# Layer 0 of a two-layer network on one Trainium2 core: the router's input of six batches turned by VectorE and DMA instead of TensorE

## The chip, the core and the metric

The kernel runs on one core of one Trainium2 chip. The core's engines work side by side, each through its own instructions in order: TensorE (PE in the profile, with its weight loads as PEld), VectorE (DVE), ScalarE (ACT), GpSimd (POOL) and SyncE (SP), which here only issues transfers (DMA). They wait for each other by semaphores. The metric is the device time of one execution in microseconds (us). Before the change it is 2221.11 us, the median of three runs (2220.45 to 2225.37).

## What is computed

Eight sequences (batches) of 512 tokens with 512 features, in f32, pass two layers. In each layer an attention and a feed-forward part follow each other, each with a residual sum and a layer norm behind it. Layer 0 alone matters here:

```python
x = L0_attn_x                                    # (8, 512, 512)
q, k, v = (x @ W.T + b for each of WQ, WK, WV)   # 16 heads of 32
attn = softmax(causal(q @ k.T / sqrt(32))) @ v
x = layernorm(x + attn @ WO.T + bO)
router_logits = x @ gate_weight.T + x @ (2 * gate_lora_B @ gate_lora_A).T   # 8 experts
weights, selected = top_k(softmax(router_logits), 2)
x = layernorm(x + sum of the two selected experts, weighted)
```

The experts' weights each have a low-rank addition (their adapters), which the kernel adds into the weights while the attention runs. Layer 1 is another attention and a quantised feed-forward part; the change does not touch it.

## The kernel before

All of layer 0's attention is in `attention0` (L1214). It walks over the eight batches `b`, in each over four groups `g` of four heads, and in each group over three units `u` of key tiles (`UNITS = ((0,), (1, 3), (2,))`): 12 units a batch, written (g, u) below. A unit is, on TensorE:

- `scores` (L1348): the products of queries and keys into one psum tile `sc` with a single buffer; ScalarE takes the exponential into `p` (L1360), GpSimd sets the masked corner to zero (L1365);
- whatever `plan` (L1410) put into this unit;
- `product` (L1370) of the unit before: `av`, four matmuls side by side for the four heads (L1380); VectorE adds the unit's `p` to the group's total (L1388);
- in a group's second unit, `normalise` (L1391) of the group before: row sums `rs` (L1395), a copy by ScalarE into `r_inv` (L995), VectorE's reciprocal (L1398) and product `aoT` (L1399), and a sum by GpSimd for a guard (L998).

`plan` is an order written by hand: a dictionary from (g, u) to the pieces to be done there. The framework's scheduler settles the order of instructions from it, for the most part as written, and moves small pieces between neighbouring ones. The pieces of batch `b`:

- `value` (L1282), `query` (L1289) and `key` (L1297): four matmuls each of 128x512, four values a batch and a query and key for each group, made a group ahead. VectorE adds the bias to the query (L1294), ScalarE to the key (L1302);
- for the batch before, `pb = b - 1`: four `project` (L1305), which multiply by WO and add to x (L1309); the last one also does the layer norm (`Env.layernorm`, L173: statistics L180 and L181, GpSimd's rstd L182 and L183, the normalising L185) and stores the rows (L188, four transfers);
- then four `turn` (L1315), each with four transposes by TensorE of 128x128 (L1320), which VectorE and ScalarE in turn copy from psum into `x1T` (L194, L192): the router needs x with the features on the partitions;
- `score` (L1326): the logits from `x1T` (L491), copied by ScalarE (L1330); `choose` (L1332): the best two experts of each token, one product (L503) and a long row of small instructions on VectorE;
- for the batch before that, `dispatch`, `one_hot` and `enter`: a table of which token goes where (L547 to L590); its one-hot rows use the same room as `x1T`, which has one buffer;
- two `merge` (L1404): two adapter products each (L781), scaled by ScalarE into buffers with the tag `r_inv` (L792), added to the expert weights by GpSimd (L794). The tag `r_inv` has two buffers, shared with the normalisation.

All psum tiles other than `sc` and `av` (v, q, k, projections, turns, logits, adapters, row sums) share the two buffers of the tag `mm`: each allocation waits until the one two before it has been copied out. SyncE loads the next batch's transposed input (L1244) and its rows x (L1248); x has two buffers, so the load for `b + 1` waits for the last reader of batch `b - 1`. GpSimd adds the bias row to x (L1474) once it has landed.

The file has a class `Turn` (L73) that layer 1's attention already uses: VectorE transposes 32x32 blocks (L88), four DMAs write them to DRAM with their blocks in another order (L93), and one DMA brings them back (L96). Its tokens then lie in another order within the batch, which `by_tile` (L98) puts right by an access pattern.

## Time and profile before

| what | value |
|---|---|
| median of the runs, us | 2221.11 |
| profiled execution, us | 2228.55 |
| its span on the core, us | 2226.8 |
| mean granted clock of TensorE | 0.993 |
| TensorE's batches 2 to 7 in the span, us each | 90.8, 93.5, 96.3, 93.5, 92.9, 93.3 |
| transposes by TensorE into `x1T` (L1320) | 128, recorded at 273 ns |
| transfers: x, 1 MB; `turned` in layer 1, 256 KB; the way back, 1 MB | 7.5, 4.1 and 4.8 us from issue to landing |

The profile is one execution taken by the hardware profiler. Its page lists the busy time of each engine; further views list waits (who waited for whom, how often and how long), instructions in order of time (start, length, engine, line, operation, output<-input, number of records) and transfers. A 128x512 matmul in f32 leaves two records. Consecutive matmuls overlap, so the sum of lengths is more than the time from the start of one to the start of the next. A batch is measured here from the first score of its first unit to that of the next batch. Layer 0's attention covers the first 760 us of the span.

### The profile page before, as it was taken

The page shows a single profiled execution, that of the slowest core. Times are in us where ns is not written, and L with a number is a line of the kernel's source. Part 1 is how long each engine was busy: PE and PEld are TensorE (multiplying, and loading weights), DVE is VectorE, ACT ScalarE, POOL GpSimd, SP SyncE. Part 2 cuts the span into 40 slices and gives each one's busy share as a digit, 9 for nine tenths or more (in the row PEclk, how much of TensorE's full clock was granted, in tenths as well). Part 3 has the DMA queues.
Part 4 walks back from the last instruction along what each step waited for, and adds up shares of the span by engine and source line. Part 5 has one row for each costly group of instructions (what it writes and reads, how often), then busy time and mean ns, then how long its engine had stood idle before and what let it go on. Part 6 is the DMA issues. An engine that isn't in the chain of part 4 may idle for free. (4 is left out here: it accounts for less than half of the span.)

```text
span 2226.8 us, 23678 instructions
## 1 busy us (share of the span) xinstructions
PE 2191.9 (98%) x9006; PEld 1116.6 (50%) x9006; DVE 1273.7 (57%) x2032; ACT 632.0 (28%) x917; POOL 487.6 (22%) x489
## 2 busy tenths in 40 slices
PE   9999999999999999999999999999999999999997
PEld 3344444444444444444443333333343778888876
DVE  3556666666666633323316887798757655555443
ACT  2332323323233232122124333223332222222222
POOL 2322423234132333122105222222211000000000
PEclk9999999999999899999999999999999999999999
DMA  8010101101022216888735212312110321111000
GB/s 297 20 57 1 57 10 48 58 1 58 5 71 94 85 57 181 227 218 214 191 114 193 80 57 86 95 55 77 45 32 13 109 78 57 57 57 57 20 20 21
DMA packets 146428, 182.20 MB, mean 82 GB/s; under 512 B 60530, under 2 KB 89202, under 8 KB 144514
## 3 DMA queue, kind: packets, MB, share of 16 engines
q1 hardware_dynamic: 135024, 144.91, 21.0%
q0 software_dynamic: 10560, 34.61, 5.5%
q8 instruction: 74, 1.21, 0.2%
q10 hardware_dynamic: 722, 1.07, 0.1%
q14 instruction: 48, 0.39, 0.1%
HBM read 117.38 MB, written 63.18 MB: 81 GB/s over the span
## 5 line engine op out<-in xcount | busy, mean ns | idle before, releaser
L903 PE MATMUL ps_gu<-experts,xrT 128*128 128x512 f32 (+1 forms) x520 | 248.8, 601 | 0.0
L1360 ACT ACTIVATE p<-sc 128x2048 f32<-128x2048 f32 (+1 forms) x96 | 152.8, 1592 | 190.0 <-PE sc L1356 183.1
L1148 DVE SCALAR_TENSOR_TENSOR hT<-ps_u,vec,sg 128x512 f32<-128x512 f32 x88 | 65.6, 745 | 195.2 <-PE ps_u L1143 195.2
L1365 POOL TENSOR_SCALAR_AFFINE_SELECT p<-p 128x512 f32<-128x512 f32 x128 | 91.6, 729 | 385.2 <-ACT p L1360 378.5
L1159 PE MATMUL ps_f<-ffn_w,h_half 128*128 128x512 f32 x672 | 170.2, 394 | 0.6 <-issue 0.4
L998 POOL TENSOR_TENSOR g_total<-g_total,r_inv 128x512 f32<-128x512 f32 x64 | 89.7, 1401 | 358.3 <-DVE r_inv L1735 283.0
L1705 ACT ACTIVATE p<-sc 128x1024 f32<-128x1024 f32 x128 | 124.0, 1021 | 105.9 <-PE sc L1702 100.8
L1735 DVE RECIPROCAL r_inv<-r_inv 128x512 f32<-128x512 f32 x32 | 107.1, 3346 | 78.8 <-ACT r_inv L995 78.8
L1388 DVE TENSOR_TENSOR p<-p 128x1536 f32<-128x1536 f32 (+2 forms) x96 | 129.4, 1348 | 39.2 <-POOL p L1365 22.2
L905 DVE TENSOR_TENSOR h<-ps_gu,h 128x256 f32<-128x256 f32 x67 | 28.4, 424 | 212.8 <-ACT h L904 212.8
L903 PEld LDWEIGHTS ps_gu<-experts,xrT 128*128 128x128 f32 x520 | 96.2, 197 | 89.7 <-issue 89.5
L1159 PEld LDWEIGHTS ps_f<-ffn_w,h_half 128*128 128x128 f32 x672 | 124.4, 188 | 33.0 <-DVE h_half L1154 5.6
L1143 PE MATMUL ps_g<-x_high,ffn_w 128*128 128x512 f32 x352 | 138.9, 395 | 0.8 <-DVE x L1676 0.8
L1143 PE MATMUL ps_g<-x_low,ffn_w 128*128 128x512 f32 x352 | 139.1, 395 | 0.0
L1143 PE MATMUL ps_u<-x_low,ffn_w 128*128 128x512 f32 x352 | 138.8, 394 | 0.0
L1143 PE MATMUL ps_u<-x_high,ffn_w 128*128 128x512 f32 x352 | 138.7, 394 | 0.0
L919 PE MATMUL ps_y<-experts,hT 128*128 128x512 f32 (+1 forms) x272 | 127.9, 593 | 0.5 <-ACT hT L913 0.5
L1702 PE MATMUL sc<-qT,kT 64*128 64x512 f32 x512 | 127.3, 615 | 1.0 <-ACT qT L1609 0.7
L1292 PE MATMUL ps_q<-experts 128*128 128x512 f32 x256 | 121.1, 615 | 4.4 <-DMA experts<-in_xT 4.4
L1724 PE MATMUL av<-p,v 128*64 128x512 f32 x512 | 123.8, 605 | 0.0
L1285 PE MATMUL ps_v<-experts 128*128 128x512 f32 x256 | 118.0, 609 | 3.3 <-DVE v L1287 3.3
L1670 PE MATMUL ps_o<-attn_out,aoT 128*128 128x512 f32 x256 | 117.9, 605 | 0.8 <-ACT r_inv L995 0.8
(262 smaller groups left out, 3438.5 us busy)
## 6 DMA issues: line engine op xcount, KB each, us to landing
results<-y SPq DMA_DIRECT2D x68, 256.0 KB, 2.3
turned<-turned SPq DMA_DIRECT2D x56, 256.0 KB, 4.1
pair<-xrT SPq DMA_DIRECT2D x25, 512.0 KB, 3.4
xrT<-pair SPq DMA_DIRECT2D x100, 128.0 KB, 4.5
x<-in_x SPq DMA_DIRECT2D x8, 1024.0 KB, 7.5
experts<-in_gate_up SPq DMA_DIRECT2D x8, 1024.0 KB, 10.8
rows<-x SPq DMA_DIRECT2D x32, 256.0 KB, 2.0
x<-rows SPq DMA_DIRECT2D x8, 1024.0 KB, 15.5
```

Source lines behind the costliest of these rows:

```text
L903: nc.tensor.matmul(ps, lhsT=xT[:, c, :], rhs=self.weights(i, c), start=c == 0, stop=c == ND - 1)
L919: self.nc.tensor.matmul(ps, lhsT=hT[:, c, :], rhs=self.weights(i, ND + c), start=c == 0, stop=c == self.NI - 1)
L1143: nc.tensor.matmul(ps, lhsT=w[:, ts(dc, P)], rhs=x[:, dc, :], start=(dc, i) == (0, 0), stop=(dc, i) == (ND - 1, 1))
L1159: self.nc.tensor.matmul(os[t], lhsT=h[:, ts(t, P)], rhs=self.weights(2 * NHID + c), start=(c, i) == (0, 0), stop=(c, i) == (NHID - 1, 1))
L1285: nc.tensor.matmul(ps, lhsT=xts[b][:, c, ts(t, P)], rhs=wv[:, c, :], start=c == 0, stop=c == ND - 1)
L1292: nc.tensor.matmul(ps, lhsT=wq[:, g, ts(c, P)], rhs=xts[b][:, c, :], start=c == 0, stop=c == ND - 1)
L1360: nc.scalar.activation(p, sc[:, :, :width], AF.Exp, scale=scale)
L1388: nc.vector.tensor_tensor(total[:, :, P * kt :], total[:, :, P * kt :], p[:, :, at : at + w], ALU.add)
L1670: nc.tensor.matmul(ps, lhsT=state[b]["aoT"][:, c, ts(t, P)], rhs=w_out[:, c, :], start=c == 0, stop=c == ND - 1)
L1702: nc.tensor.matmul(sc[:, j, :], lhsT=st["kT"][hs, ts(kt, P)], rhs=st["qT"][g][hs, :], start=True, stop=True)
L1705: nc.scalar.activation(p, sc, AF.Exp, scale=scale)
L1724: nc.tensor.matmul(st["av"][HD * j : HD * (j + 1), :], lhsT=st["v"][:, kt, HD * j : HD * (j + 1)], rhs=p[:, j, :], start=kt == 0, stop=kt ...
```

## The change

Batches 0 to 5 (`by_blocks = NB - 2`) no longer use `turn`. A new `blocks(b)` does what layer 1 does: four block transposes by VectorE into `x1T`, four DMAs to DRAM and one back into the same tile. The logits of these batches are put in the old order of tokens by the access patterns of ScalarE's copy. Batches 6 and 7 are turned by TensorE as before.

The pieces are laid out anew in the plans of batches 1 to 6 (`by_dma`), each of which treats the batch before it:

- projections: from (1,0), (1,0), (1,1), (1,2) to (1,0), (1,1), (1,2), (2,0);
- turning: from two pieces in (2,1) and two in (2,2) to `blocks` in (2,1);
- logits from (3,0) to (3,1), choice from (3,1) to (3,2);
- adapters ("merge"): from ahead of the other pieces in (2,0) and (3,0) to behind the key in (2,2) and behind the logits in (3,1);
- the next batch's first query: from (3,1) to (3,0).

The query of the fourth group in batches 1 to 6 gets its bias from ScalarE instead of VectorE. On SyncE's queue the five new transfers follow the stores of the rows; the load of the next batch's x stands between the four writes and the way back.

```diff
@@ query
-            nc.vector.tensor_scalar(q, ps, vec[:, V_BQ + g : V_BQ + g + 1], None, ALU.add)
+            if g == ND - 1 and 0 < b <= by_blocks:
+
+                nc.scalar.activation(q, ps, AF.Identity, bias=vec[:, V_BQ + g : V_BQ + g + 1])
+            else:
+                nc.vector.tensor_scalar(q, ps, vec[:, V_BQ + g : V_BQ + g + 1], None, ALU.add)
...
+        by_blocks = NB - 2
+        turns = Turn(env, dram, NT, "turned0")
+
+        def room(b):
+            x1Ts[b] = work.tile([P, ND, S], F32, tag="x1T", name="x1T")
+
+        def blocks(b):
+            room(b)
+            flat = x1Ts[b].rearrange("p k s -> p (k s)")
+            for t in range(NT):
+                turns.blocks(flat, t, xs[b][:, t, :])
+            turns.out(flat)
+            turns.back(flat)
...
@@ score
-            nc.scalar.copy(logits[b], ps)
+            if b < by_blocks:
+                nc.scalar.copy(turns.by_tile(logits[b], False), turns.by_tile(ps, True))
+            else:
+                nc.scalar.copy(logits[b], ps)
...
@@ plan
+            pb, last = b - 1, b == NB - 1
+            by_dma = 0 <= pb < by_blocks
...
-                    todo[g, 1].append(lambda nb=nb, ng=ng: query(nb, ng))
+                    todo[g, 0 if by_dma and ng == 0 else 1].append(lambda nb=nb, ng=ng: query(nb, ng))
...
-                places = ((1, 0), (1, 0), (1, 1), (1, 1) if last else (1, 2))
+                places = ((1, 0), (1, 1), (1, 2), (2, 0)) if by_dma else ((1, 0), (1, 0), (1, 1), (1, 1) if last else (1, 2))
...
-                places = ((2, 0),) * 4 if last else ((2, 1), (2, 1), (2, 2), (2, 2))
-                for c, slot in enumerate(places):
-                    todo[slot].append(lambda c=c: turn(pb, c))
-                todo[(2, 1) if last else (3, 0)].append(lambda: score(pb))
-                todo[(2, 2) if last else (3, 1)].append(lambda: choose(pb))
+                if by_dma:
+                    todo[2, 1].append(lambda: blocks(pb))
+                else:
+                    for c in range(ND):
+                        todo[2, 0].append(lambda c=c: turn(pb, c))
+                todo[(3, 1) if by_dma else (2, 1)].append(lambda: score(pb))
+                todo[(3, 2) if by_dma else (2, 2)].append(lambda: choose(pb))
                 if not last:
-                    todo[2, 0].append(merge)
-                    todo[3, 0].append(merge)
+                    todo[2, 2 if by_dma else 1].append(merge)
+                    todo[3, 1].append(merge)
```

The transfers it calls:

```python
    def out(self, room):
        for i in range(self.N):
            src = room[32 * i : 32 * (i + 1), :].rearrange("r (k j f) -> r k j f", j=self.N, f=self.n * 32)
            self.nc.sync.dma_start(out=self.dram.rearrange("(j r) k i f -> r k j i f", j=self.N)[:, :, :, i, :], in_=src)

    def back(self, room):
        self.nc.sync.dma_start(out=room, in_=self.dram.rearrange("p k i f -> p (k i f)"))
```

More of the change, by code (lines that the diff above doesn't have):

```diff
@@ L1313, in attention0 @@
         x1Ts, logits = {}, {}
+        by_blocks = NB - 2
[9 more added lines that the diff above has]
+            turns.back(flat)
         def turn(b, c):
             if c == 0:
-                x1Ts[b] = work.tile([P, ND, S], F32, tag="x1T", name="x1T")
+                room(b)
             ps = mm([P, S], "ps_x1T")
@@ L1417, in plan @@
                 if nb < NB:
-                    todo[g, 1].append(lambda nb=nb, ng=ng: query(nb, ng))
+                    todo[g, 0 if by_dma and ng == 0 else 1].append(lambda nb=nb, ng=ng: query(nb, ng))
                     todo[g, 2].append(lambda nb=nb, ng=ng: key(nb, ng))
-            pb, last = b - 1, b == NB - 1
             if b:
-                places = ((1, 0), (1, 0), (1, 1), (1, 1) if last else (1, 2))
+                places = ((1, 0), (1, 1), (1, 2), (2, 0)) if by_dma else ((1, 0), (1, 0), (1, 1), (1, 1) if last else (1, 2))
                 for t, slot in enumerate(places):
                     todo[slot].append(lambda t=t: project(pb, t))
-                places = ((2, 0),) * 4 if last else ((2, 1), (2, 1), (2, 2), (2, 2))
-                for c, slot in enumerate(places):
-                    todo[slot].append(lambda c=c: turn(pb, c))
-                todo[(2, 1) if last else (3, 0)].append(lambda: score(pb))
-                todo[(2, 2) if last else (3, 1)].append(lambda: choose(pb))
+                if by_dma:
[5 more added lines that the diff above has]
+                todo[(3, 2) if by_dma else (2, 2)].append(lambda: choose(pb))
                 if not last:
-                    todo[2, 0].append(merge)
-                    todo[3, 0].append(merge)
+                    todo[2, 2 if by_dma else 1].append(merge)
+                    todo[3, 1].append(merge)
             if b == 0:
```

## The prediction

> **What bounds the kernel now.** I read the page first, for the share of each engine; then TensorE's waits in the first 760 us, which hold layer 0's attention; then the timelines of one batch, engine by engine. The page:

> ```profile
> PE 2191.9 (98%) x9006; PEld 1116.6 (50%) x9006; DVE 1273.7 (57%) x2032; ACT 632.0 (28%) x917; POOL 487.6 (22%) x489
> ```

> TensorE's waits in 0 to 760 us (total, times, longest):

> ```profile
> PE sc L1356 <- ACT p L1360: 5.2, 7, 1.8
> PE ps_q L1292 <- DMA experts<-in_xT: 4.4, 1, 4.4
> PE ps_v L1285 <- DVE v L1287: 3.3, 4, 1.7
> ```

> The reader sees 98% and, in 760 us, waits of a few us: here the end moves with what TensorE is given, plus the waits a change makes. The fourth batch (267 to 364 us), where the third one's rows are turned; columns are start, length, engine, line, operation and records:

> ```profile
> 327.82 1.14 PE L1356 MATMUL sc<-q,k 32*128 32x512 f32 x8
> 328.78 1.02 PE L781 MATMUL ps_lora<-lora 16*128 16x512 f32 x4
> 329.74 0.64 PE L1380 MATMUL av<-p,v 128*32 128x256 f32 x8
> 330.96 1.15 PE L1356 MATMUL sc<-q,k 32*128 32x384 f32 x16 [0.58 <-ACT p L1360]
> 332.04 3.70 PE L1292 MATMUL ps_q<-experts 128*128 128x512 f32 x8
> 335.57 0.60 PE L1320 MATMUL ps_x1T<-ident,x 128*128 128x128 f32 x4
> 336.10 1.04 PE L1380 MATMUL av<-p,v 128*32 128x512 f32 x2
> 337.08 0.66 PE L1320 MATMUL ps_x1T<-ident,x 128*128 128x128 f32 x4
> ...
> 343.70 0.60 PE L1320 MATMUL ps_x1T<-ident,x 128*128 128x128 f32 x4
> 344.23 0.83 PE L1380 MATMUL av<-p,v 128*32 128x384 f32 x2
> 344.99 0.66 PE L1320 MATMUL ps_x1T<-ident,x 128*128 128x128 f32 x4
> 345.58 1.06 PE L1380 MATMUL av<-p,v 128*32 128x384 f32 x14
> ```

> Tails overlap, so I take costs from start to start. The turns also split the products (av): two records alone take 0.98 us (336.10 to 337.08), while all eight of an unbroken set, at 317.26, take 0.88.

> **What goes.** In unit (2,1) (second of the three units of the third head group) turns, products and sums run from 335.57 to 339.51, 3.94 us; the same products and sums unbroken, in unit (1,1), 317.26 to 319.11, 1.85. The turns cost 2.09. In (2,2) it is 343.70 to 346.57, 2.87, against 326.82 to 327.82, 1.00: 1.87. Together 3.96 us a batch, of which only 2.24 are the turns themselves (0.53 + 0.59, twice). In the built order a projection of 3.53 us stands in (2,0) between that unit's scores and the next, so the wait of 0.58 at 330.96 goes too.

> [...]

> **What moves on TensorE.** Projections, the next batch's query, logits and the choice's product (0.89) keep their lengths. The second adapter pair breaks the scores of (3,1) now (1.92 us instead of 1.08) and breaks that unit's products afterwards. I take the same 0.84; from nothing to 1.1, the larger break in (2,1), is possible, so the ends are +0.8 and -0.3 us. The first pair goes behind the key in (2,2): its second product needs the psum buffer of that key, two allocations back, and ScalarE frees it 0.69 us (k rows) after the key ends, while the first adapter takes 0.48 and the copy starts some 0.2 late: a new wait of about 0.45. So 3.96 + 0.58 - 0.45 = 4.1; adding whole units the same way gives 3.95. I use **4.0 us a batch, 24 in six**.

> **What must hide.** I set the batch's clock to 0 at the start of unit (1,0), 298.66 in the trace. Units afterwards: (1,0) 5.2, (1,1) 11.7, (1,2) 8.7, (2,0) 5.2, (2,1) 6.5, (2,2) 6.7, (3,0) 5.2. So the last projection ends at 30.2, (3,1) begins at 49.2, and its logits want the turned rows at **50.2**.

> The way to them: add, statistics, mean 1.63 us (327.53 to 329.16 before), 1.47 until rstd is there; normalising starts at 33.4. Next, the rows from VectorE's timeline, the first of this batch, the others in layer 1:

> ```profile
> 330.63 4.14 DVE L185 TENSOR_SCALAR x<-x,mv,rstd 128x512 f32<-128x512 f32 x4 [1.48 <-POOL rstd L183]
> ...
> 1258.20 1.92 DVE L746 TENSOR_SCALAR xn<-x,mv,dev 128x512 f32<-128x512 f32 x4
> 1260.03 2.48 DVE L88 STREAM_TRANSPOSE turned<-xn 128x512 f32<-128x512 f32 x4
> ```

> The 4.14 lie beside GpSimd's two adapter sums (2.84 us from 331.65), which move away; two masks (1.22) stay. So 1.9 to 4.1, likely 2.9; blocks 2.5 to 2.7. They end at 37.8 to 40.2, likely 38.9. Then SyncE's queue, as layer 1 does the same transfers:

> ```profile
> 1262.54 3.26 SPq L93 DMA_DIRECT2D turned<-turned  x4
> 1269.11 0.35 SPq L96 DMA_DIRECT2D hT<-turned  x1
> ```

> Four writes, then the way back 6.6 us after the first; it lands 4.8 later (median of its issues), so 11.4 after the blocks. Here the next batch's 1 MB load of x is issued between the two. It lands 5.2 to 7.5 us after issue elsewhere, moving its bytes in about 3. At 343.89 and 345.68 two such loads ran one after the other, so I let x follow the writes: it is done some 9.3 after the blocks and pushes the return by 0.4. Landing is 11.8 after the blocks: 49.6 to 52.0, likely 50.7. The logits wait 0 to 1.8, likely 0.3 to 0.5 (I take 0.3, the nearer to the rows without GpSimd). Behind that wait on TensorE stand the adapters, products and sums of (3,1) and the whole next batch.

> **Other queues.** VectorE loses a query copy (0.75) and two copies of turned rows (1.36) and gains the blocks: +0.4 to 0.6 us a batch in 93, idle for a third of it. What lies behind the blocks is the add (1.7 to 2.1), the reciprocal (3.34) and GpSimd's sum (1.5) that frees r_inv for the second scaled adapter. That ends at about 45.5, ScalarE copies until 46.2, then the exponential of (3,0) takes 1.88: 48.1, and the scores of (3,1) want it at 49.2. One us of cover; if it is gone, a late normalising costs the scores what it would cost the logits, not both. ScalarE loses two copies (0.59 each) and gains the query (0.69); the reordering logits copy has no row: between the plain 0.58 and twice that, with a quarter product in front of the waiting adapter; 0 to 0.6 a batch, I take 0 as the plain copy is the same size. On GpSimd the addition to x (4.53) begins when x has landed, 48.7 instead of 54.7 on this clock; masks and adapter sums follow until 55.9, and the sums' copy, wanted at 55.1, is a us late as it was before (1.79 <-POOL experts at 359.18), with a key of 3.5 behind it as cover. The choice comes one unit later and ends VectorE's chain at about 68.2 on the clock; the values that want its copy come at 70.9. Before, the copy was late by 0.55 behind this batch and by 1.7 ahead of it; I count neither back. SyncE's other issues are behind the return: the load of xT, at 45.2 before and 46 now, needed a batch later.

> **Sum.** 6 x (4.0 - 0.3) = 22.2 us. The profiled execution took 2228.55 us around a span of 2226.8: 2204.6 for the span, 2206.4 for the run. It lies 7.4 above the median of the runs, 2221.11, which I move by the same amount: **2199 us**.

> **Rivals.** (A) The forecast, 2193 to 2205: waits of 0 to 1.3 a batch give 16 to 24 us back, and 3 to 4 more if the value waits shrink. For it: a TensorE that hardly waits loses work. Chance 0.60. (B) The turned rows land late by 1.5 to 3 us: normalising takes its 4.14, or x and the writes share. Of 4.0 a batch 1 to 2.5 stay, 6 to 15 us: 2206 to 2215, 2211 in the middle. For it: the return's place behind x; against it: two loads in turn at 343.89. Chance 0.20. (C) Slower. One mechanism: x's load is mixed with the writes, so the return is issued only after both. Blocks at 40.2, 1.2 to the first packet, 5 + 3 of transfer, 0.7 to the issue, 4.8 to land: 54.9, a wait of 4.7 that eats the 4.0. The deciding point is a landing after 54.2 on the clock, 14 to 16.4 behind the blocks; that gives 2225, and 2232 with another us a batch. Chance 0.10. (D) The turns were no loss: the units run into the exponentials instead, as batch 0's thin units do (3.55 us for 1.7 of products), and the time stays at 2217 to 2225. Against it: every unit of the new order has 3.5 us of projection, query or key beside its scores, except (3,1). Chance 0.07. (E) Also the value waits and the broken sets go: below 2193, 0.03.

> **Range and chances.** A and B hold 0.8: 2193 to 2215. A measurement here can tell 0.2% from no change, 4.4 us. Faster A, B, E: 0.83; same, D: 0.07; slower, C: 0.10.

> **What would show it.** In the profile after: 32 turns by TensorE instead of 128; TensorE's batches of 89 to 90 us instead of 93; the blocks ending near 39 and the normalising near 3 us; the return landing 11 to 12 behind the first write; TensorE's wait of the logits on that DMA under a us. A wait there of 2 us or more is B, of 4 or more C; new waits of scores on exponentials are D. The prediction is wrong if x's load holds up the return, or if normalising stays at 4.1.

## The result and the profile after

The changed kernel takes 2256.41 us (median of four runs, 2252.91 to 2260.69) against 2222.85 of the kernel before on the same chip: a ratio of 1.0152 with a 95% interval of 1.0137 to 1.0168. It is slower, by 1.5%; the forecast was 2199, at most 2215. The profiled execution took 2258.85 us around a span of 2257.0. From its page:

```profile
PE 2206.0 (98%) x8910; PEld 1104.9 (49%) x8910; DVE 1261.8 (56%) x2038; ACT 632.1 (28%) x911; POOL 492.6 (22%) x489
PEclk9999899999999999999999999999999999999999
```

TensorE does 96 instructions fewer and is busy for 14 us more. So its work did not grow, it got slower: the clock row shows an 8 (mean clock 0.981, before 0.993). TensorE's waits in 0 to 800 us:

```profile
PE ps_logits L491 <- DMA x1T<-turned: 18.2, 6, 3.4
PE ps_q L1292 <- DMA experts<-in_xT: 4.5, 1, 4.5
PE ps_lora L781 <- DVE first_h L905: 2.9, 1, 2.9
```

The first line is new: in all six batches the logits wait for the way back, 3.0 us on average. That is 18 us, about what the forecast wanted to gain, but not yet a loss of 34. TensorE's timeline of the fifth batch shows the rest:

```profile
461.21 1.06 PE L491 MATMUL ps_logits<-x1T,r_wr 128*32 128x512 f32 x8 [3.25 <-DMA x1T<-turned]
462.20 1.38 PE L781 MATMUL ps_lora<-lora 16*128 16x512 f32 x2
463.51 1.92 PE L1401 MATMUL av<-p,v 128*32 128x512 f32 x2
...
468.23 2.76 PE L1416 MATMUL rs<-p,ones 128*32 128x512 f32 x7
```

Two records of the products take 1.92 us and seven of the row sums 2.76. The same forms in the fourth batch of before:

```profile
336.10 1.04 PE L1380 MATMUL av<-p,v 128*32 128x512 f32 x2
338.14 1.44 PE L1395 MATMUL rs<-p,ones 128*32 128x512 f32 x7
```

The stage after by stretches: start:end and length, then busy us and records of PE, PEld, DVE, ACT and POOL, then the granted clock, the DMA share and GB/s:

```profile
459.53:462.94 3.41, 1.73 (x10) 0.48 (x10) 0.00 (x0) 1.02 (x2) 3.41 (x1) 1.00 0.78 305
462.94:473.18 10.24, 10.24 (x29) 2.35 (x29) 3.11 (x2) 2.84 (x5) 3.92 (x5) 0.50 0.00 1
473.18:476.59 3.41, 3.41 (x13) 1.74 (x11) 3.41 (x4) 0.31 (x2) 1.96 (x2) 1.00 0.00 0
```

The clock is 0.50 for 10.24 us, starting 1.7 us behind the end of the wait. Each of the six waits has such a stretch at its end or behind it, of 6.83 to 13.65 us: 61.4 us at half clock. Half of that, an estimated 30.7 us, was lost.

### The profile page after: what moved, and what is told of

Same layout as the page of the kernel before. It is cut to its first block, busy times and chain, and to the rows that moved or that the text cites. A ratio compares the mean times of both kernels' runs of the same rounds, so it can differ in the third digit from the quotient of the medians.

```text
span 2257.0 us, 23548 instructions
## 1 busy us (share of the span) xinstructions
PE 2206.0 (98%) x8910; PEld 1104.9 (49%) x8910; DVE 1261.8 (56%) x2038; ACT 632.1 (28%) x911; POOL 492.6 (22%) x489
## 5 line engine op out<-in xcount | busy, mean ns | idle before, releaser
L1292 PE MATMUL ps_q<-experts 128*128 128x512 f32 x256 | 120.7, 613 | 4.5 <-DMA experts<-in_xT 4.5
L1304 PE MATMUL ps_k<-experts 128*128 128x512 f32 x256 | 119.1, 608 | 0.2 <-ACT r_inv L995 0.2
## 6 DMA issues: line engine op xcount, KB each, us to landing
x<-rows SPq DMA_DIRECT2D x8, 1024.0 KB, 15.1
```

The source lines that it names most:

```text
L1292: nc.tensor.matmul(ps, lhsT=wq[:, g, ts(c, P)], rhs=xts[b][:, c, :], start=c == 0, stop=c == ND - 1)
L1304: nc.tensor.matmul(ps, lhsT=wk[:, g, ts(c, P)], rhs=xts[b][:, c, :], start=c == 0, stop=c == ND - 1)
```

## The experiments

The table counts TensorE's batches 2 to 7, as in the table of before: their sum, TensorE's waits ahead of the logits in them, and the time at clock 0.50 between 82 and 690 us of the span. These three come from the one profiled execution of each kernel; times are medians of all its executions, ratios are against the kernel before on the same chip.

| kernel | us | ratio (95%) | batches 2-7 | logits wait | half clock |
|---|---|---|---|---|---|
| before | 2222.85 | | 560.2 | | 3.4 |
| after | 2256.41 | 1.0152 (1.0137-1.0168) | 590.6 | 18.2 | 61.4 |
| e1, x behind | 2237.85 | 1.0057 (1.0041-1.0074) | 569.2 | 4.7 | 20.5 |
| e2, no way back | 2209.95 | 0.9939 (0.9922-0.9955) | 543.0 | 0 | 0 |
| e3, 4 useless ahead | 2224.11 | 0.9999 (0.9989-1.0009) | 557.3 | 0 | 0 |
| e9, 2 useless ahead | 2222.10 | 0.9993 (0.9982-1.0005) | 555.0 | 6.1 | 3.4 |
| e14, 1 useless ahead | 2231.32 | 1.0024 (1.0008-1.0040) | 563.7 | 10.6 | 23.9 |
| e17, 4 useless behind | 2245.51 | 1.0095 (1.0069-1.0120) | 576.3 | 16.5 | 13.7 |
| e18, adapters first alone | 2211.01 | 0.9946 (0.9930-0.9963) | 541.0 | 5.8 | 0 |
| e19, GpSimd's add later alone | 2259.80 | 1.0176 (1.0150-1.0202) | 587.2 | 18.6 | 54.6 |
| e16, e18 and e19 together | 2213.69 | 0.9955 (0.9938-0.9972) | 542.0 | 6.9 | 0 |
| e15, as e16, with x behind | 2208.88 | 0.9928 (0.9907-0.9949) | 539.4 | 4.3 | 0 |

Theory W, formed from the two traces: the way back lands late because x's load is ahead of it; the logits wait; behind the wait TensorE runs at half clock, which costs more than the wait. Rivals: the new layout itself costs TensorE time; or another engine holds (3,1).

**e2: without the way back.** The line `turns.back(flat)` is left out, so the logits of six batches are those of unpermuted blocks.

> The way back from DRAM is left out, so the router's logits of six batches come from rows that are turned only within 32x32 blocks; TensorE, VectorE, ScalarE and the four writes do the same work as after the change. Theory W: no wait of the logits, no stretch at clock 0.5 there, 2197 to 2206 us: what the change is worth without its wait. Rival R: narrow products and order stay, so the clock still falls and the time is 2235 or more. Rival D: the writes stay and the return (1 MB of 3) goes: 2235 to 2250.

2209.95 us, 4 above W's range. Without the transfer there is no wait and no half clock, and the layout gains. The account of the loss then closes to 1.3 us: from 543.0 to 590.6 are 47.6 us, and waits of 18.2 plus half the 61.4 make 48.9. Missed is the size of the gain: 17.2 us in the six batches, 5.2 of which are value waits in (0,1) that vanish (10.87 to 10.0 us on average). That leaves 2.0 us a batch, where the forecast had 4.0.

**e3, e9, e14: useless matmuls ahead of the logits**, which fill the wait with work (0.88 us each; n = 4, 2, 1):

```diff
+            if b < by_blocks:
+                fill = mm([P, S], "ps_fill")
+                for c in range(n):
+                    nc.tensor.matmul(fill, lhsT=wq[:, 0, ts(c, P)], rhs=wo[:, c, :], start=c == 0, stop=c == n - 1)
             ps = mm([P, S], "ps_logits")
             router.logits(x1Ts.pop(b), ps)
```

> After the change, with four useless 128x512 products (3.5 us) on TensorE ahead of the logits of six batches; nothing reads them. Theory W: the wait is filled, the granted clock stays at 1.0 behind it, so about 3.5 us a batch are lost instead of 3.0 of wait and some 5 of half clock: 2217 to 2230 us, faster than after the change although 21 us of work are added. Rivals R and D: the work is added to a loss that stays, 2256 or more.

> The changed kernel with two useless 128x512 matmuls (1.77 us) ahead of the logits of batches 0 to 5, where four took the wait and the clock dips away (2224.11 us). The wait left should be 1.0 to 1.5 us a batch. If such a wait leaves the clock alone, six batches cost about what they do with four: 2219 to 2226. If it halves the clock for 3.4 us (1.7 us lost) a batch: 2229 to 2236. If the half clock does not hang on the wait's length but on there being one: 2248 or more.

> The changed kernel with one useless matmul ahead of the logits (none: waits of 2.4 to 3.4 us, dips of 6.8 to 13.7 us behind each; two: waits of 1.0, one dip of 3.4 us in six). Waits of 1.8 to 2.2 us should be left. If the clock falls by the length of the wait, some dips of 3.4 to 6.8 us remain: 2226 to 2245. If every wait over 1.5 us costs as much as the full one: 2248 or more. If the limit is above 2.2 us: 2219 to 2226.

With four, 21 us of useless work in the six batches make the kernel 32 us faster: the wait was no longer idle time, and the clock stayed up. That is the plainest proof that the half clock, and not the wait, was the larger loss. With two, waits of 0.64 to 1.33 us remain and one stretch of 3.41 us at half clock follows a 1.30. With one, the waits are 1.58, 1.48, 1.92, 2.10, 1.75, 1.80 and the half clock follows the last three alone. So there is no sharp length: 1.92 went free and 1.75 did not. The three times lie in the first range of their expectations.

**e17: the same four matmuls behind the logits.**

> The changed kernel with four useless matmuls behind the logits instead of ahead of them (ahead: 2224.11 us, no wait, no dips). The wait of about 3 us stays. If idle TensorE brings the half clock, whatever follows: dips of 6.8 to 13.7 us behind each of the six, and 2256 plus 21, about 2270 to 2290, as the filler runs in part at half clock. If it is the narrow work behind the wait (adapters of 16 rows, products of 32 columns) that keeps the clock down: dips of 3.4 us or none, and 2255 to 2268.

2245.51 us: below both theories' numbers, and 11 us faster than the changed kernel in spite of 21 us of useless work. The waits stay (2.45 to 3.51), but only three of six have a half clock behind them, 3.4 or 6.8 us long:

```profile
446.20:449.61 3.41, 1.56 (x24) 0.72 (x16) 0.70 (x1) 1.72 (x1) 2.04 (x2) 1.00 0.98 378
449.61:456.44 6.83, 6.10 (x13) 2.08 (x14) 0.00 (x0) 0.74 (x2) 3.88 (x3) 0.50 0.29 110
```

So a wait alone does not bring it (one of 2.69 went free here, while one of 2.42 in the changed kernel did not); what follows the wait has a part in whether it comes and how long it lasts: behind 128x512 matmuls 13.7 us in all, behind adapters of 16 rows and products of 32 columns 61.4. The waits themselves are 1.6 us shorter in sum, a small part of that.

**e1: x's load behind the way back** (SyncE's order written out by hand, the load issued after `turns.back`).

> The load of the next batch's x is issued behind the way back (SyncE's order held as written in layer 0); everything else as after the change. Theory W (a late return: x's bytes pass the queue ahead of it, TensorE waits 2.4 to 3.4 us for the logits, and the granted clock is 0.5 for some 10 us behind each such wait): the return lands about 11.4 us after the blocks instead of 15.1, the wait of the logits falls to 0 to 0.6 us, the stretches at clock 0.5 behind it go, and the time is 2199 to 2212 us; GpSimd's addition to x starts some 2 us later, which can make the row sums' copy late and cost up to 1.8 us a batch. Rival R (the new order is what slows: narrow adapter and logits products and broken sets lower the clock whatever is waited for): clock 0.5 stays behind the logits, 2235 us or more. Rival D (the transfers themselves slow TensorE): the same bytes move, so little changes, 2245 or more.

2237.85 us, far above W's 2199 to 2212: 20 of the 34 us of loss are gone. The logits wait 0.4 to 1.5 us. But GpSimd's addition of the bias row to x, 4.53 us, starts when x has landed, now later, and the adapter sums behind it come late; the row sums' copy needs their buffers:

```profile
PE ps_r L503 <- ACT r_inv L995: 10.9, 6, 2.0
```

Behind these waits of up to 2.0 us the clock is at half again. To take GpSimd's addition away from there, GpSimd's order was written out by hand and the addition moved to the batch that comes next:

```diff
-                    nc.gpsimd.tensor_tensor(xs[b], xs[b], row[:, 1:2, :].to_broadcast([P, NT, D]), ALU.add)
...
                     p = scores(b, g, u)
+                    if u == 2 and g == (2 if b == 0 else 0):
+                        nc.gpsimd.tensor_tensor(xs[b], xs[b], row[:, 1:2, :].to_broadcast([P, NT, D]), ALU.add)
```

**e6 and e7** put it at the start of the batch, ahead of the mask of (0,0), e7 with x's load behind the way back; **e10** is e7 with the lines above, behind the mask of (0,2).

> GpSimd's instructions in program order, with the addition to the next batch's x at the start of that batch instead of in front of the masks of (3,1); nothing else changes. Theory W (TensorE's wait for the way back of the rows and the half clock behind it): nothing of that is touched, the logits wait about 3 us in each of six batches, the clock dips stay, and the time stays at 2248 to 2260. Rival P (GpSimd's 4.53 us in front of masks and adapter sums is what makes (3,1) long): the masks come 4.5 us earlier, (3,1) falls from 14 to 16 us to under 10, and the time is 2215 to 2235.

> Both: the load of x behind the way back of the rows, and GpSimd's addition to x a batch's group later. If the two things left in the kernel with x behind (2237.85 us) are GpSimd's late adapter sums, with the row sums' copy behind them, and the clock that falls after the wait of 2 us they cause: no wait of 1.5 us or more is left, no dips between 82 and 690 us, batches of 91 to 92 us as in the kernel without the way back (90.85), and 2209 to 2217 us, faster than the kernel before the change. Rival: something else holds (3,1) and (3,2) back there, batches stay at 94 to 96 and the time at 2230 to 2240.

> As the kernel with both edits (2240.47 us), but GpSimd's addition to x stands behind the mask of (0,2), not ahead of the mask of (0,0). If its loss was the values' wait on the choice (15.6 us in six, 2.6 each, with a half clock of 3.4 us behind most) because VectorE's sums waited for masks behind that addition: (0,0) falls from 13.2 to 8.7 us, no dips between 82 and 690 us, the logits wait 0.5 to 1.6 as there, and the time is 2209 to 2219. Rival: the choice is late whatever GpSimd does, since it is one unit later in the new order, and the values wait as before: 2232 or more.

e6: 2268.57 us (1.0203, 1.0182 to 1.0225), above W's 2260. W's wait stays, as W said (17.2 us, half clock behind all six), and 9.5 us of a new wait come, the values for the choice. e7: 2240.47 (1.0080, 1.0057 to 1.0103), a miss: the new wait is 15.6 us, (0,0) takes 13.2 us instead of 8.7. e10: 2228.05 (1.0020, 1.0009 to 1.0032), above its range too: (0,0) is back at 8.7, but (1,1) takes 13.14 instead of 11.74, with 1.1 us of wait for a projection's addition by VectorE. The reason stands in the timelines of VectorE and GpSimd (of e12, where it is the same):

```profile
380.02 5.54 DVE L1410 TENSOR_TENSOR p<-p 128x1024 f32<-128x1024 f32 x1 [0.55 <-POOL p L1387]
```

```profile
379.96 4.52 POOL L1514 TENSOR_TENSOR x<-x,row 128x2048 f32<-128x2048 f32 x1
```

A sum that takes 1.22 us at 407.50 of that timeline takes 5.54 beside GpSimd's addition and ends a full 1.1 us behind it. 4.52 plus 1.22, less the 0.06 that VectorE started later, are 5.68: an estimate, from these rows, of a sum done only behind the addition.

**e12: e10 with the adapters of (3,1) ahead of the logits** (two lines change places in the plan). **e15** is e12 with GpSimd's addition behind the mask of (1,2), where VectorE has room. **e16** is e15 with x's load ahead of the way back again. **e18** is the changed kernel with the two lines alone, **e19** with GpSimd's addition alone.

```diff
-                todo[(3, 1) if by_dma else (2, 1)].append(lambda: score(pb))
-                todo[(3, 2) if by_dma else (2, 2)].append(lambda: choose(pb))
                 if not last:
                     todo[2, 2 if by_dma else 1].append(merge)
                     todo[3, 1].append(merge)
+                todo[(3, 1) if by_dma else (2, 1)].append(lambda: score(pb))
+                todo[(3, 2) if by_dma else (2, 2)].append(lambda: choose(pb))
```

> As behind_and_late, with the adapters of (3,1) ahead of the logits instead of behind them. The logits are wanted about 1.1 us later (an adapter product and a quarter of the products), so their wait falls from about 1.0 to 0 to 0.4 a batch, no dips: 2205 to 2214. Rival: the second adapter's scale or the row sums become late instead, and the time is that of behind_and_late or more.

> As adapter_first (2215.74 us), with GpSimd's addition to x behind the mask of (1,2) instead of (0,2). There a sum of VectorE took 5.54 us beside that addition (1.22 without it), so a projection came 1.1 us late in five batches and (1,1) took 13.14 us instead of 11.74. If VectorE stands still beside the addition: (1,1) is back at 11.74, batches 90.2, time 2207 to 2211. Rival: the lock only moves to the projection's add or the statistics of (2,0), a new wait of 1 us or more shows there, and the time stays at 2213 to 2218.

> As late_in_1_2, but with the load of x ahead of the way back as in the changed kernel: the place of the load alone. If the load ahead costs the way back about 2.2 us (waits of 3.0 against 0.8 us), the logits, now wanted 1.1 us later, wait 1.5 to 2.2 us in each of six batches, and the clock halves behind some of them: 2220 to 2240. Rival: adapters ahead of the logits and GpSimd's place are all that is needed, and the load's place costs nothing: 2207 to 2213.

> The changed kernel with one edit: the adapters of (3,1) ahead of the logits; load of x and GpSimd's addition as changed. With both edits beside it the time was 2213.69 us. If GpSimd's addition, which starts when x has landed, holds the masks of (3,0) and (3,1) up to some 2 to 3 us longer than the way back: the products, now in front of the logits, wait 1 to 2.5 us for masks in most batches, some dips stay, 2222 to 2242. If the order of logits and adapters was all: 2210 to 2217.

> The changed kernel with one edit: GpSimd's addition to x behind the mask of (1,2) of the next batch; load of x ahead and logits first as changed. If the way back is what the logits wait for: waits of about 3 us and the dips stay, 2246 to 2259. If GpSimd's addition beside the transfers made the wait or the dips: 2215 to 2235.

e12: 2215.74 us (0.9962, 0.9950 to 0.9974), slightly above its range, since the wait of 1.1 us in (1,1) stays and the second adapter's buffer costs 0.7 ahead of the logits. e15: 2208.88; (1,1) is back at 11.74 and every batch from the third on takes 90.25, as expected. e16: 2213.69, with waits of 0.9 to 1.8 and no half clock, 6 us under the range expected and just above the rival's: the place of x's load is worth 5 us at most once the logits come later. e19: 2259.80, no better than the changed kernel (waits of 3.1 us on average, half clock behind five of the six; the sixth, of 2.19, went free). e18 fell where the order was to be all: **2211.01 us**, 45 us faster than the changed kernel by two lines in another order. Its profiled execution took 2205.41, the other three 2210.99 to 2211.36, so the others (mean clock 0.993 to 0.995, here 0.996) may hold some half clock that this profile does not show. Its waits, and TensorE's timeline:

```profile
PE ps_logits L491 <- ACT scaled L792: 3.4, 4, 1.2
PE ps_logits L491 <- DMA x1T<-turned: 2.5, 2, 1.4
```

```profile
430.60 1.03 PE L781 MATMUL ps_lora<-lora 16*128 16x512 f32 x4
431.56 1.05 PE L1401 MATMUL av<-p,v 128*32 128x512 f32 x2
434.04 1.07 PE L491 MATMUL ps_logits<-x1T,r_wr 128*32 128x512 f32 x8 [1.43 <-DMA x1T<-turned]
434.89 0.59 PE L1416 MATMUL rs<-p,ones 128*32 128x512 f32 x1
```

Adapters and a quarter of the products, 2.0 us from 430.60 to 432.6, now stand in the time of the wait, and the products and row sums behind the logits run at their usual 0.6 to 1.05. The expectation feared GpSimd's masks behind its addition; the masks of (3,1) are indeed done only at 437, but their products come in the next unit, at 441.8. With e19, which moves the addition away and gains nothing, the addition was not the cause in the changed kernel.

**e5, e8, e11: the new layout with the turns back on TensorE**, two pieces in (2,1) and two in (2,2); e8 with GpSimd's addition as in e6, e11 as in e10.

> The new order with the turns back on TensorE: the four turns in (2,1) and (2,2), plain logits copy, no transfers of turned rows; query on ScalarE, projections, adapters, logits and choice where the change puts them. Theory W: no wait, no clock loss; the order alone is worth about 0 to 0.6 us a batch: 2217 to 2224 us. Rival R: the order carries the loss: 2240 or more. Rival D: as before the change, 2217 to 2224.

> The new order of pieces with the turns back on TensorE (2256.41 us before), and GpSimd's addition to x at the start of the next batch. If the masks behind that addition (waits of 1.1 to 1.9 us in seven places) and the clock behind those waits made that kernel slow: no wait on the masks, no dips, batches of 93 to 95 us (90.85 of the kernel without the way back plus 2 to 4 for the turns), time 2219 to 2233. Rival: the new order costs TensorE time in itself (breaks of sets, waits for turned rows): 2240 or more.

> The new order with the turns on TensorE and GpSimd's addition behind the mask of (0,2). The order alone, without its GpSimd waits: batches of 94 to 96 us (the earlier version's 98.8 to 102.3 less 4.5 for the values' wait and what the clock cost), time 2225 to 2238, so somewhat over the kernel before; against the kernel without the way back (90.85 a batch) this gives what the turns cost TensorE in this order. Rival: the order is as good as the old one, 93.3 a batch and 2217 to 2224.

2256.41 (1.0137, 1.0120 to 1.0154), 2266.14 (1.0193, 1.0171 to 1.0216), 2251.76 (1.0121, 1.0096 to 1.0146). The first two lie where their rival stood, that the new order costs TensorE time in itself, and the third above both its ranges. So for turns on TensorE that rival holds, at least in part; for the changed kernel it does not, since e2 has its order, its blocks and no loss. The layout without the blocks is a loss: in e11, (2,1) takes 9.54 us (6.56 with the blocks) and (3,0) 7.6 to 9.3 (5.27), because the adapters that follow the key wait for a turned row's copy and stand inside the scores of (3,0). In the fourth batch (here of e11) the clock falls there though TensorE hardly idles:

```profile
352.87:356.28 3.41, 3.06 (x13) 1.00 (x13) 1.18 (x2) 1.02 (x3) 0.34 (x1) 1.00 0.99 352
356.28:359.69 3.41, 3.41 (x5) 1.37 (x5) 0.00 (x0) 1.84 (x2) 2.74 (x3) 0.50 0.42 163
```

In the first stretch TensorE is 3.06 of 3.41 us busy, much of it with scores of 32 rows and adapters of 16. What brought the half clock there no run separates.

## Why the prediction was wrong

- **Units up to (3,0)**: right. (1,0) 5.27, (1,1) 11.74, (1,2) 8.71, (2,0) 5.27, (2,1) 6.56, (3,0) 5.27, against 5.2, 11.7, 8.7, 5.2, 6.5, 5.2. (2,2) took 7.17 instead of 6.7.
- **Normalising and blocks**: right. VectorE's lines after, in the same batch:

```profile
441.05 2.56 DVE L185 TENSOR_SCALAR x<-x,mv,rstd 128x512 f32<-128x512 f32 x4 [1.48 <-POOL rstd L183]
443.53 2.48 DVE L88 STREAM_TRANSPOSE x1T<-x 128x512 f32<-128x512 f32 x4
```

 With (1,0) at 406.8, the blocks end at 39.2 on the batch's clock; forecast 38.9.
- **"Landing is 11.8 after the blocks"**: this step failed. It was 15.1. SyncE's lines, then issue to landing:

```profile
446.04 3.79 SPq L93 DMA_DIRECT2D turned<-x1T  x4
449.99 1.25 SPq L1248 DMA_DIRECT2D x<-in_x  x1
453.59 0.33 SPq L96 DMA_DIRECT2D x1T<-turned  x1
```

```profile
turned<-x1T SPq DMA_DIRECT2D x4, 256.0 KB, 4.2
x<-in_x SPq DMA_DIRECT2D x1, 1024.0 KB, 8.6
x1T<-turned SPq DMA_DIRECT2D x1, 1024.0 KB, 7.5
```

 The way back is issued 7.5 us after the first write (6.6 in layer 1), and lands 7.5 after that, not 4.8 + 0.4. The forecast took x's megabyte as done 9.3 behind the blocks; it landed at 12.6: its packets came after those of the writes, whose last ended 7.0 behind the blocks, and the last of them ran beside those of the way back. The forecast wrote that such loads land 5.2 to 7.5 us after issue; its view of before gives 5.2, 7.5 and 15.0 as least, median and most, and the six loads in this stage reach 8.7. With x behind (e1) the way back was issued just as late, 7.5, and the logits began 5.1 after it: 12.7 behind the blocks. So x's place costs about 2.5 us and the slower writes 0.9.
- **"The logits wait 0 to 1.8, likely 0.3 to 0.5"**: it was 2.4 to 3.4, from the step above. That is B by its wait and C by its landing (15.1 lies in C's 14 to 16.4), though not by C's mechanism: the way back was issued at 453.59, five us before x had landed. The forecast's own sign of being wrong, x's load holding up the return, came true. But B put the time at 2206 to 2215 and C at 2225 to 2232.
- **The price of a wait**: this step failed too, and it weighs most. A, B and C took a wait at its own length; the half clock behind it stood at nothing, without a reason. The runs show 18.2 us of waits and 61.4 us at half clock behind them, an estimated 30.7 lost. The row that could have warned was there: the trace of before has 3.4 us at half clock right behind the 1.7 us of its value wait. In the runs waits from 1.30 us on (e9) had half clock behind them in places, and in e11 so had a stretch of 3.41 us that was 0.90 busy.
- **"4.0 us a batch"**: mis-sized. It was 2.0 (e2): the seven units that lose or gain pieces, (1,0) and (2,0) to (3,2), take 42.6 us there and 44.6 before, where the forecast's units leave 40.7. Of the missing 2.0, 1.2 are in (3,1): its adapters stand between the parts of its products and it takes 7.0 without any wait, not the 5.8 or so that the forecast's sum leaves for it (e3, where they follow the useless matmuls in one piece, takes 9.38, less four of 0.88: 5.9). So the break did not keep its price of 0.84 when it moved from scores to products. Another 0.5 is in (2,2). With the adapters first the seven units take 42.3 (e18). The value waits, which only the best part of A and E counted, gave 5 us back.
- **GpSimd's sums** and the exponentials of (3,0): covered, as forecast; no wait in the changed kernel's batches 2 to 7 names them.
- **"The turns were no loss" (D)**: false. Its sign, new waits of scores on exponentials, did not come: there were seven before (5.2 us in 0 to 760 us), and one is left (1.8, in the last batch, as before). Without the way back (e2) the layout gains 2.0 us a batch.

Together: the waits cost 16 us more than the 1.8 forecast, the half clock an estimated 31, the gain was 12 smaller, and the value waits gave 5 back; that is 54 of the 57 us between 2199 and 2256.

## What to carry to other kernels

Price a wait of TensorE by what it does to the clock, not by its length: where waits of 1.5 to 3.9 us were followed by narrow matmuls, the half clock, taken at half its length, cost an estimated 1.1 (e14) to 1.7 times (the changed kernel) their sum again, and where they were mostly under 1.5 us there were 3.4 us (e9) and none (e16) of it. Before a transfer replaces work of TensorE, look at what can stand ahead of its consumer in TensorE's own order; here 2.0 us of adapters and products put ahead of the logits turned a loss of 34 us into a gain of 13, where moving the transfer that held up the rows gave 19 of those 45 us.
